# Two attention layers on one core: layer 1's q and k by seven products of quarters in 20 of 24 head pairs

## The chip, the cores and the metric

The kernel runs on one core of one Trainium2 chip. The metric is the device time of one execution in microseconds, the median of three runs. All data are 32-bit floats in SBUF; matrix products and the adds that make their inputs are in this type too.

## The reference, cut to what matters

Two layers run one after the other on an image batch of 4 x 32 x 32 tokens and 768 channels (12 heads of 64). Each normalizes its input by groups, computes q, k and v for every token, attends over all 1024 tokens with two position biases, projects, and adds the result to its input. Layer 1 also convolves q, k and v with a 3x3 depthwise kernel and normalizes each head:

```python
qkv = x @ w_qkv.T + b_qkv
q, k, v = (qkv[0], qkv[1], qkv[2])          # per head, H x W x 64
q = layer_norm(dwconv3x3(q, w_pool_q), g_q, b_q)
k = layer_norm(dwconv3x3(k, w_pool_k), g_k, b_k)
v = layer_norm(dwconv3x3(v, w_pool_v), g_v, b_v)
attn = einsum('bqc,bkc->bqk', q * scale, k) + rel_h[..., None] + rel_w[..., None, :]
o = softmax(attn) @ v + q
x = x + o @ w_proj.T + b_proj
```

The change is in the first line, for q and k of layer 1 alone.

## The kernel before

**Stages and pairs.** A stage is one batch image in one layer. The eight stages run in the order: layer 0 of images 0 and 1, layer 1 of images 0 and 1, then the same for images 2 and 3 (L170). A stage has six pairs of heads (hp 0 to 5), so there are 48 items; items 12 to 23 and 36 to 47 are layer 1. A pair fills 128 partitions, two heads of 64. Tokens are cut in two halves of 512.

**Steps.** `attend` (L735) is the frame. For one pair it goes through two halves of queries, and in each through two groups of four key tiles. A group computes four score tiles "s" (L915 for q and k, L917 for the position bias), ScalarE takes the exponentials "e" (L922), and then TensorE multiplies them with the values ("av", L939). It yields twice after the scores and twice after av, so one pair's attention has 16 steps: steps 0, 1, 4, 5, 8, 9, 12, 13 come after scores, the others after av. All other work is tied to steps by the table `events` (L1088): `plan` (L650) gives each pair's pieces with a step relative to the attention of the pair before it, and negative steps lie in the attention two before. At one step, pieces of earlier pairs come first. Each engine works its queue strictly in this program order.

**Layer 1's preparation of a pair** (L682 to L724): `padded` computes one half of q, k or v by 12 matmuls of 64 columns (`product`, L469; `halves`, L134, splits 128 columns in two; each matmul is two instructions in the profile) and ScalarE copies it with its bias into a padded image (two copies, L534). q's halves come at steps -7 (-8 for hp 1 and 4) and -6, k's at -4 and -2, v's at 2 and 4. VectorE (DVE) then convolves with nine taps (L549 the first, L551 the others): q's taps at steps -4 to 0, k's at 2 to 6, v's at 8 to 11. `centre` (L553; q at 3, k at 8, v at 13) transposes on TensorE ("ln_c"), and DVE subtracts the mean (L566, L567). `norm` (q at 7 or 8, k at 12, v at 15) takes the reciprocal root on ScalarE (L159, L161) with a step of Newton on DVE (L163 to L166) and multiplies (L589); for v the result is "vt", which av reads. `back` (q at 9, k at 14) transposes again ("ln_t") and ScalarE writes q and k. `positions` (L605, steps 10 and 11) computes the position terms "rel", and ScalarE copies them; `split` (L631, step 12) makes the bias out of them: ScalarE rounds (L636), DVE takes the rest (L637), and GpSimd sends 16 DMAs (L647).

**PSUM.** Eight banks: two for the first and fourth score tiles, one for av, one small bank, and two places of two banks, left ("b") and right ("c"), that hold the second and third score tiles. Other work takes single banks from the places in a fixed turn: after scores left, left, right, right; after av right, right, small, left, left (L118, L125). A new tile waits until all readers of what lay there are done.

**Weights and DMA.** `load_weights` (L247) has two buffers; `used` (L271) asks for the use after the next when one is done, on the queue of SyncE (SP). The order of uses is the list `uses` (L223).

**Products by sevens** exist already in layer 0 (`sevens`, L398) and in the projections (`four` and `three`), with sums of weights made once by DVE (`mix_weights`, L274) and kept in DRAM ("mixed").

**Projection and group norm.** The projection of a stage runs inside the first attention of the next, on steps 9 to 19 when layer 1 follows (L1138). The group norm of the next stage (L312) runs at given steps after the first of the stage before (L1099).

Of the kernel before, what the change touches and what calls it, by code (L numbers as in the profile page):

```python
# [51 lines left out]
def two_layers(ctx: ExitStack, tc: tile.TileContext, keep, x_in, wqkv, wproj, rels, windows, vrow, small, const, onehot, picks, out):  # L52
# [81 lines left out]
    def halves(ps, a, b, start=True, stop=True, **kw):  # L134

        for lo in (0, D):
            nc.tensor.matmul(ps[lo : lo + D], a[:, lo : lo + D], b, start=start, stop=stop, **kw)  # L137
# [37 lines left out]
    def rows(x):  # L175
# [3 lines left out]
    weights = {}  # L179

    N_SUMS = 5
    V_SUMS, PROJ_SUMS = NC, NC + NC // 2
    mixed = [
        dram.tile([P, N_SUMS, NC // 2, P], F32, tag=f"mixed{u}", name=f"mixed{u}")
        for u in range(PROJ_SUMS + 2 * (NC // 2))
    ]
    mixed_there = set()


# [19 lines left out]
    def in_sevens(i):  # L209

        return items[i][1] == 0 and i >= 2

    def shift(i):

        return 4 if i and items[i][1] == 0 and items[i - 1][1] == 1 else 0
# [8 lines left out]
    for i, (_, layer, hp) in enumerate(items):  # L224
        first = (i - 1) * 16 + shift(i)
        if in_sevens(i):
            uses += [(first, (i, 0, 0)), (first + 0.1, (i, 0, 1)), (first + 2, (i, 0, 2)), (first + 2.1, (i, 0, 3))]
            if hp % 2 == 0:
                uses += [(first + 8, (i, 2, 0)), (first + 8.1, (i, 2, 1)), (first + 10, (i, 2, 2)), (first + 10.1, (i, 2, 3))]
        else:  # L230
            uses += [(first + r, (i, s)) for s, r in enumerate((-8, -4, 2) if layer else (0, 4, 8))]
    uses = [use for _, use in sorted(uses)]
# [14 lines left out]
    def load_weights(n):  # L247

        if n >= len(uses):
            return  # L250
        i, s, *some = uses[n]
        _, layer, hp = items[i]
        w = wp.tile([P, NC, P], F32, tag="wqkv", name="wqkv_t")
        weights[uses[n]] = w
        if not some:
            nc.sync.dma_start(w, wqkv[layer, hp, :, s])
        elif some[0] == 0:
            (pa, sa), (pb, sb) = two(i, s)
            nc.sync.dma_start(w[:, :3, :], wqkv[0, pb, :, sb, 3:])
            nc.sync.dma_start(w[:, 3:, :], wqkv[0, pa, :, sa, :3])  # L260
        else:
            load_sums(w, hp if s == 0 else V_SUMS + hp // 2, some[0])
# [11 lines left out]
    def mix_weights(u):  # L274


        a = wp.tile([P, NC, P], F32, tag="wproj", name="mix_a")
        b = wp.tile([P, NC, P], F32, tag="wproj", name="mix_b")
        if u < PROJ_SUMS:
            (pa, sa), (pb, sb) = two(u, 0) if u < V_SUMS else two(2 * (u - V_SUMS), 2)  # L280
            nc.sync.dma_start(a, wqkv[0, pa, :, sa])
            nc.sync.dma_start(b, wqkv[0, pb, :, sb])
        else:
            layer, m = divmod(2 * (u - PROJ_SUMS), NC)
            for i, w in enumerate((a, b)):
                nc.sync.dma_start(w, wproj[layer, :, :, m + i, :].rearrange("h p q -> p h q"))
        yield
        a1, a2, b1, b2 = a[:, :3, :], a[:, 3:, :], b[:, :3, :], b[:, 3:, :]
        for n, to, x, y, op in (
            (2, None, a1, b2, ALU.add), (4, None, b1, a1, ALU.subtract), (0, b1, b1, b2, ALU.add),  # L290
            (1, a1, a1, a2, ALU.add), (3, a2, a2, b2, ALU.subtract),
        ):
            if to is None:
                to = wp.tile([P, HALF], F32, tag="x", name="mix")
                to = to[:, : 3 * P].rearrange("p (n c) -> p n c", c=P)
            nc.vector.tensor_tensor(to, x, y, op)
            nc.sync.dma_start(mixed[u][:, n], to)
        mixed_there.add(u)
        yield

    def mix_tokens(stage):


        x11, x12, x21, x22 = (xns[stage][:, n : n + 3, h : h + HALF] for n in (0, 3) for h in (0, HALF))
        for to, x, y, op in (
            (quarters[2], x21, x22, ALU.add), (x21, x21, x11, ALU.subtract), (quarters[1], x11, x12, ALU.add),
            (x12, x12, x22, ALU.subtract), (quarters[0], x11, x22, ALU.add),
        ):
            nc.vector.tensor_tensor(to, x, y, op)
            yield  # L310

    def group_norm(stage):  # L312
# [69 lines left out]
    class Pair:  # L382
# [9 lines left out]
        def column(self, s):  # L392
            return BIAS[self.layer] + 6 * s + self.hp

        def make_vt(self):
            self.vt = work.tile([P, NKT, P], F32, tag="vt", name="vt")

        def sevens(self, s, second):  # L398

# [107 lines left out]

        def put_k(self, ps, h, scale, bias):
            if self.k is None:
                self.k = work.tile([P, T], F32, tag="k", name="k")  # L510
            nc.scalar.activation(self.k[:, h * HALF : (h + 1) * HALF], ps, AF.Identity, bias=bias, scale=scale)

        def plain(self, s, h):
# [10 lines left out]
        def padded(self, s, h):  # L524

            if h == 0:
                self.pad[s] = in_turn("pad", pads)
            ps = self.product(s, h)
            ps = ps.rearrange("p (a c) -> p a c", a=S)

            for g, own, there in ((h, slice(0, S // 2), 1), (1 - h, slice(-1, None) if h == 0 else slice(0, 1), 0 if h == 0 else S // 2 + 1)):
                src = ps[:, :, own]
                rows = slice(g * (S + 2) + 1, g * (S + 2) + 1 + S)
                nc.scalar.activation(  # L534
                    self.pad[s][:, rows, there : there + src.shape[2]], src, AF.Identity, bias=col(self.column(s))
                )

        def taps(self, s, lo, hi):

            n_rows = 2 * S + 2  # L540
            if lo == 0:

                self.y[s] = in_turn("y", convolved)
            y = self.y[s].rearrange("p (a c) -> p a c", c=S // 2)
            for t in range(lo, hi):
                window = self.pad[s][:, t // 3 : t // 3 + n_rows, t % 3 : t % 3 + S // 2]
                tap = col(TAPS + 9 * s + t)
                if t == 0:
                    nc.vector.tensor_scalar(y, window, tap, None, ALU.mult)  # L549
                else:  # L550
                    nc.vector.scalar_tensor_tensor(y, window, tap, y, ALU.mult, ALU.add)  # L551
# [98 lines left out]
        def plan(self):  # L650
# [14 lines left out]
            if not self.layer:  # L665
# [15 lines left out]

            late = self.hp in (0, NC // 2)  # L682
            early_late = self.hp in (1, NC // 2 + 1)
            pieces = [
                (-8 if early_late else -7, lambda: self.padded(Q, 0)),
                (-6, lambda: self.padded(Q, 1)),
                (-4, lambda: self.padded(K, 0)),
                (-2, lambda: self.padded(K, 1)),
                (2, lambda: self.padded(V, 0)),
                (4, lambda: self.padded(V, 1)),  # L690
                (3, lambda: self.centre(Q)),
# [19 lines left out]

            taps = (
                (Q, -4, (2, 2, 2, 2, 1)),
                (K, 2, (2, 2, 2, 2, 1)),
                (V, 8, (2, 2, 3, 2)),
            )
            for s, r, counts in taps:
                lo = 0
                for n in counts:
                    some = lambda s=s, lo=lo, n=n: self.taps(s, lo, lo + n)  # L720
                    some.taps = True
                    pieces.append((r, some))
                    r, lo = r + 1, lo + n
# [371 lines left out]
    for k in range(1, len(stages)):  # L1095
        first = (k - 1) * NC * n_steps
        at(first + n_steps + 4, lambda k=k: load_xn(stages[k]))
        norm = group_norm(stages[k])
        for r in (34, 37, 41, 41, 48, 48, 52, 55, 58, 61, 64) if stages[k - 1][1] else range(34, 70, 3):  # L1099
            at(first + r, lambda norm=norm: next(norm, None))  # L1100
        if stages[k][1] == 0:
            mix = mix_tokens(stages[k])
            for r in range(5):
                step = 5 * n_steps + r // 3 if stages[k - 1][1] else 4 * n_steps + 4 + r // 2
                at(first + step, lambda mix=mix: next(mix, None))
        elif stages[k - 1][1] == 0:
            at(first + 4 * n_steps + 6, lambda: [nc.gpsimd.memset(pad, 0.0) for pad in pads])
# [3 lines left out]

    for u, call, step in (
        (2, 0, 5), (7, 6, 11), (3, 13, 18), (4, 22, 29), (8, 31, 38), (5, 40, 47), (0, 49, 55), (6, 57, 63), (1, 65, 71),
        (9, 72, 77), (10, 78, 83), (11, 84, 89), (12, 124, 135), (13, 137, 147), (14, 149, 159),
    ):
        mix = mix_weights(u)
        for at_step in (call, step):
            at(at_step, lambda mix=mix: next(mix))
# [6 lines left out]
    for k, stage in enumerate(stages):  # L1125
# [6 lines left out]
            continue  # L1132
        at(first + 2, call)
        late = stages[k + 1][1]
        for r, what in ((1, (0,)), (6, (1,)), (8, (2,)), (9, (3,)), (10, (4,))) if late else ((4, (0, 1)), (5, (2,)), (6, (3,)), (8, (4,))):
            at(first + r, lambda sums=sums, what=what: sums(what))

        for r, n in zip((9, 11, 13, 15, 17, 19) if late else (7, 9, 11, 13, 14, 15), (2, 1) * 3):  # L1138
# [339 lines left out]
```

## Time and profile before

| | |
|---|---|
| median of three runs | 3781.18 us (3780.49 to 3783.07) |
| profiled execution | 3784.75 us |
| its span, first to last instruction | 3783.0 us |
| granted TensorE clock | 0.998 |
| PE (TensorE) busy | 3730.7 us, 99% |
| DVE busy | 2397.2 us, 63% |
| ACT (ScalarE) busy | 1654.9 us, 44% |
| POOL (GpSimd) busy | 624.9 us, 17% |
| one pair of layer 1, 1323.8 to 1396.3 | 72.5 us: PE 72.5, DVE 55.6, ACT 36.2 |

The profile is one execution. Rows of groups give line, engine, operation, what is written from what, shapes and count; then busy time and the mean of one in ns; then the engine's idle time ahead of these instructions and who ended it. Timeline rows give start, duration, engine, line and operation, and idle time before in brackets. PEld is TensorE's loading of weights, which overlaps its matmuls. "Busy" of PE is modelled from pipelined matmuls.

### The profile page before, as it was taken

To read this page: it belongs to the slowest core of one execution; us is meant where nothing else is said; L and a number is where in the kernel's file an instruction comes from. 1 tells how busy PE (TensorE), PEld (TensorE's weight loads), DVE (VectorE), ACT (ScalarE), POOL (GpSimd) and SP (SyncE) were. 2 spreads that over 40 slices of the span, in tenths; PEclk is the share of its full clock that TensorE was granted. 3 is DMA by queue.
4 is the path that set the end of the run, shared out by engine and by line. 5 is a ranking of instruction groups with operands and counts; after the bars stand their busy time and mean duration, and the time that the engine had idled before them with its cause. 6 is when DMAs were issued, how large, how long until landed. Compare 5 with 4: busy or idle time off the path is not lost.

```text
span 3783.0 us, 77367 instructions
## 1 busy us (share of the span) xinstructions
PE 3730.7 (99%) x33166; PEld 1655.8 (44%) x33166; DVE 2397.2 (63%) x3069; ACT 1654.9 (44%) x2338; POOL 624.9 (17%) x1152
## 2 busy tenths in 40 slices
PE   8999999999999999999999999999999999999998
PEld 4535535534344444444535445355343444434442
DVE  2566554559678777688444554445686787867774
ACT  2455424545245443345424544254442554524551
POOL 0111100110122221122300010011111122111230
PEclk9999999999999999999999999999999999999999
DMA  4444543431431223411344232523224222142123
GB/s 149 115 134 124 144 143 102 113 90 46 123 100 48 64 57 94 127 49 47 88 120 128 62 86 67 182 68 86 55 54 142 71 64 58 47 127 66 47 59 101
DMA packets 209166, 345.08 MB, mean 91 GB/s; under 512 B 36982, under 2 KB 93202, under 8 KB 208816
## 3 DMA queue, kind: packets, MB, share of 16 engines
q1 hardware_dynamic: 130832, 224.84, 19.2%
q0 software_dynamic: 77984, 115.21, 13.1%
q8 instruction: 264, 4.33, 0.5%
q14 instruction: 86, 0.70, 0.1%
HBM read 195.95 MB, written 43.09 MB: 63 GB/s over the span
## 4 chain that ended last, share of the span: by engine, by line
PE 91%; DVE 5%; issue 1%; DMA 1%; ACT 1%; POOL 0%; SPq 0%; DVEq 0%; ACTq 0%; POOLq 0%
PE qkv L137 20%; PE s L915 17%; PE av L939 16%; PE m1m L137 5%; PE m4m L137 4%; PE m3m L137 4%; PE s L917 4%; PE p4p L137 3%; PE p3p L137 3%; PE rel L620 3%; PE p1p L137 3%; PE m L137 2%; PE ln_c L563 2%; PE p L137 1%; DVE acc L933 1%
## 5 line engine op out<-in xcount | busy, mean ns | idle before, releaser
L922 ACT ACTIVATE e<-s 128x1024 f32<-128x1024 f32 x768 | 775.3, 1023 | 407.7 <-PE s L917 377.8
L137 PE MATMUL qkv<-xn,wqkv_t 128*64 128x512 f32 x3648 | 814.4, 595 | 4.5 <-PE ln_t L598 2.4
L915 PE MATMUL s<-q,k 64*128 64x512 f32 x3072 | 809.0, 603 | 2.8 <-ACT e L922 1.9
L551 DVE SCALAR_TENSOR_TENSOR shared<-shared,sm 128x1056 f32<-128x1056 f32 x576 | 757.2, 1315 | 14.5
L917 PE MATMUL s<-bias,ones 64*128 64x512 f32 x1536 | 614.7, 791 | 1.4 <-issue 0.7
L939 PE MATMUL av<-e,vt 128*64 128x512 f32 x2624 | 597.9, 597 | 0.0
L647 POOL DMA_DIRECT2D bias<-high x384 | 203.5, 552 | 1750.7 <-ACT high L636 1484.0
L137 PEld LDWEIGHTS qkv<-xn,wqkv_t 128*64 128x64 f32 x3648 | 256.2, 137 | 479.8 <-issue 465.7
L933 DVE TENSOR_TENSOR acc<-acc,e 128x1024 f32<-128x1024 f32 x294 | 360.1, 1225 | 123.0 <-ACT e L922 96.1
L915 PEld LDWEIGHTS s<-q,k 64*128 64x128 f32 x3072 | 280.0, 186 | 260.7 <-issue 217.3
L534 ACT ACTIVATE shared<-qkv,sm 128x512 f32<-128x512 f32 (+1 forms) x288 | 129.0, 501 | 546.1 <-PE qkv L137 528.3
L939 PEld LDWEIGHTS av<-e,vt 128*64 128x64 f32 x2624 | 186.3, 137 | 349.6 <-issue 314.1
L917 PEld LDWEIGHTS s<-bias,ones 64*128 64x128 f32 x1536 | 149.8, 187 | 183.6 <-issue 180.8
L647 POOL DMA_DIRECT2D bias<-whole x384 | 206.9, 569 | 25.5 <-DVE whole L637 14.8
L762 ACT COPY weighed<-av 128x512 f32<-128x512 f32 x96 | 56.3, 587 | 307.8 <-PE av L939 307.8
L931 DVE TENSOR_TENSOR acc<-e 128x1024 f32<-128x1024 f32 x49 | 60.0, 1224 | 165.4 <-PE z L837 126.2
L566 DVE TENSOR_REDUCE mean<-ln_c 128x8 f32<-128x512 f32 x144 | 98.6, 685 | 101.1 <-PE ln_c L563 101.1
L780 POOL DMA_DIRECT2D inv<-z_inv x94 | 55.2, 592 | 592.1 <-DVE z_inv L774 543.9
L620 PEld LDWEIGHTS rel<-q,rel 64*32 64x32 f32 x6144 | 111.9, 105 | 60.6 <-issue 56.5
L620 PE MATMUL rel<-q,rel 64*32 64x32 f32 x6144 | 122.6, 195 | 1.9 <-issue 1.9
L620 PE MATMUL rel<-q_t,rel 64*32 64x32 f32 x6144 | 123.6, 195 | 0.2 <-issue 0.2
L419 DVE TENSOR_TENSOR shared<-shared,m3m 128x512 f32<-128x512 f32 x66 | 45.3, 687 | 121.7 <-PE m3m L137 121.7
(177 smaller groups left out, 4312.1 us busy)
## 6 DMA issues: line engine op xcount, KB each, us to landing
bias<-high POOLq DMA_DIRECT2D x384, 128.0 KB, 2.9
bias<-whole POOLq DMA_DIRECT2D x384, 128.0 KB, 3.1
wqkv_t<-in_wqkv SPq DMA_DIRECT2D x78, 384.0 KB
wqkv_t<-mixed SPq DMA_DIRECT2D x66, 384.0 KB
wproj_t<-mixed SPq DMA_DIRECT2D x48, 384.0 KB
wqkv_t<-in_wqkv SPq DMA_DIRECT2D x66, 192.0 KB
xn<-in_x SPq DMA_DIRECT2D x24, 512.0 KB
x<-in_x SPq DMA_DIRECT2D x48, 256.0 KB
```

What stands on the lines that cost most here:

```text
L137: nc.tensor.matmul(ps[lo : lo + D], a[:, lo : lo + D], b, start=start, stop=stop, **kw)
L534: nc.scalar.activation(self.pad[s][:, rows, there : there + src.shape[2]], src, AF.Identity, bias=col(self.column(s)))
L551: nc.vector.scalar_tensor_tensor(y, window, tap, y, ALU.mult, ALU.add)
L563: nc.tensor.transpose(ps[:, t * P : (t + 1) * P], y[:, tokens], ident)
L566: nc.vector.tensor_reduce(of, heads, AX.X, ALU.add)
L620: nc.tensor.matmul(ps[lo : lo + S, k * S : (k + 1) * S].rearrange("p (b c) -> p b c", b=2), rel[rows, 2 * self.layer + i, first : first + ...
L647: nc.gpsimd.dma_start(sets, some.unsqueeze(1).to_broadcast([D // 2, 2, QC]))
L915: nc.tensor.matmul(ps[:, j, :], k[rows, keys], q[rows, cols], start=True, stop=False)
L917: nc.tensor.matmul(ps[:, j, :], ones[rows, kt % 2 * P : (kt % 2 + 1) * P], bias[c][rows, kt // 2, :], start=False, stop=True,)
L922: nc.scalar.activation(e, ps, AF.Exp)
L933: nc.vector.tensor_tensor(acc, acc, e, ALU.add)
L939: nc.tensor.matmul(av[j * D : (j + 1) * D, :], pair.vt[:, kt, j * D : (j + 1) * D], e[:, j, :], start=(kt == 0), stop=(kt == NKT - 1),)
```

## The change

For the 20 items of layer 1 whose two predecessors are layer 1 too (14 to 23, 38 to 47), q and k of a pair, both token halves, are computed together by seven products of quarters (in Strassen's manner, the form with few additions): a term is 6 matmuls, half a `padded` product. `products(0)` to `products(3)` stand where the four `padded` stood. The terms are w1, w6, (w2,) w7, w4 for q's halves, w5 and w3 for k's. Four inputs are sums of tokens (S1 to S4), made once per stage by DVE (`sum_tokens`, 12 additions of 512 columns and as many stores of 256 KB) and kept in DRAM; each pair calls each of them back, three blocks of 256 KB, into one set of buffers right after the term that read the set before. Sums of weights for the six pairs are made once (six more units of `mix_weights`, in layer 0).

The results are put together by DVE, partly in PSUM (w4, w5 and w3 get their terms added in place), before ScalarE pads them as before (`put_from` is the second half of `padded`). The first tap of k and v is done by ScalarE, at steps 1 and 6. The buffers vt and k have one place each in layer 1 now; the blocks and temporaries lie in those that layer 0 uses. The group norms ahead of layer 1 run some 10 steps earlier, and the mixing of weights is put at other steps.

The core of the diff:

```diff
+    def in_products(i):
+        return all(items[k][1] == 1 for k in (i, i - 1, i - 2))
...
+        elif in_products(i):
+            uses += [(first + r, (i, 0, n)) for n, r in enumerate((-8, -6.5, -6, -2))] + [(first + 2, (i, 2))]
         else:
             uses += [(first + r, (i, s)) for s, r in enumerate((-8, -4, 2) if layer else (0, 4, 8))]
...
+        elif layer and some[0] < 2:
+            nc.sync.dma_start(w[:, :3, :], wqkv[layer, hp, :, 0, 3 * some[0] : 3 * some[0] + 3])
+            nc.sync.dma_start(w[:, 3:, :], mixed[LATE_SUMS + hp][:, some[0]])
+        elif layer and some[0] == 3:
+            nc.sync.dma_start(w[:, :3, :], wqkv[layer, hp, :, 1, 3:])
+        elif layer:
+            load_sums(w, LATE_SUMS + hp, some[0])
...
+        if u >= LATE_SUMS:
+            t1, t2 = (
+                wp.tile([P, HALF], F32, tag="x", name="mix")[:, : 3 * P].rearrange("p (n c) -> p n c", c=P) for _ in range(2)
+            )
+            for n, to, x, y in ((3, t1, b1, a1), (0, t2, b2, t1), (1, b1, b2, b1), (2, a2, a2, t2)):
+                nc.vector.tensor_tensor(to, x, y, ALU.subtract)
+                nc.sync.dma_start(mixed[u][:, n], to)
+            mixed_there.add(u)
+            yield
+            return
...
+    def sum_tokens(stage):
+        for n in range(NC // 2):
+            x11, x12, x21, x22 = (xns[stage][:, n + k, h : h + HALF] for h in (0, HALF) for k in (0, 3))
+            def keep_sum(which, x, y, op):
+                to = wp.tile([P, HALF], F32, tag="x", name="token_sum")
+                nc.vector.tensor_tensor(to, x, y, op)
+                nc.sync.dma_start(tokens[stages.index(stage) % 2][which, n], to)
+                return to
+            s1 = keep_sum(S1, x21, x22, ALU.add)
+            s2 = keep_sum(S2, s1, x11, ALU.subtract)
+            yield
+            keep_sum(S4, x12, s2, ALU.subtract)
+            yield
+            keep_sum(S3, x11, x21, ALU.subtract)
...
+            self.vt = one.tile([P, NKT, P], F32, tag=self.home("vt"), name="vt")
...
+        def call(self, which):
+            if which == S2:
+                two_blocks = one.tile([P, 2, HALF], F32, tag="vt0", name="blocks")
+                third_block = work.tile([P, 2, QC], F32, tag="acc", name="third_block", bufs=1)
+                self.blocks = [two_blocks[:, 0], two_blocks[:, 1], third_block[:, 0]]
+            for n, block in enumerate(self.blocks):
+                nc.sync.dma_start(block, tokens[stages.index((self.b, self.layer)) % 2][which, n])
+        def seven(self, ps, at, x, more=False):
+            w = weights[self.i, 0, at // 2][:, 3 * (at % 2) : 3 * (at % 2) + 3, :]
+            for n in range(3):
+                halves(ps, w[:, n, :], x[n], start=not (n or more), stop=n == 2, skip_group_check=True)
+        def second(self):
+            self.seven(self.w12, 2, [xns[self.b, self.layer][:, 3 + n, :HALF] for n in range(3)], more=True)
+            self.put_from(0, 0, self.w12)
+        def products(self, n):
+            Q, K = 0, 1
+            xn = xns[self.b, self.layer]
+            x = {(h, k): [xn[:, 3 * k + n, h * HALF : (h + 1) * HALF] for n in range(3)] for h in range(2) for k in range(2)}
+            add = lambda to, x, y: nc.vector.tensor_tensor(to, x, y, ALU.add)
+            early = self.hp in (1, NC // 2 + 1)
+            if n == 0:
+                temps = one.tile([P, 2, HALF], F32, tag="k0", name="temps")
+                self.u, self.x = temps[:, 0], temps[:, 1]
+                self.pad[Q] = in_turn("pad", pads)
+                self.w12, w6 = bank("w1w2"), bank("w6")
+                self.seven(self.w12, 0, x[0, 0])
+                nc.scalar.copy(self.u, self.w12)
+                self.seven(w6, 1, self.blocks)
+                used((self.i, 0, 0))
+                self.call(S3)
+                if early:
+                    self.second()
+                add(self.u, self.u, w6)
+            elif n == 1:
+                w7 = bank("w7")
+                if not early:
+                    self.second()
+                self.seven(w7, 3, self.blocks)
+                used((self.i, 0, 1))
+                self.call(S1)
+                add(self.x, self.u, w7)
+                w4 = bank("w4")
+                self.seven(w4, 4, x[1, 1])
+                add(w4, w4, self.x)
+                self.put_from(Q, 1, w4)
+            elif n == 2:
+                self.pad[K] = in_turn("pad", pads)
+                w5 = bank("w5")
+                self.seven(w5, 5, self.blocks)
+                used((self.i, 0, 2))
+                self.call(S4)
+                add(self.u, self.u, w5)
+                add(w5, w5, self.x)
+                self.put_from(K, 1, w5)
+            else:
+                w3 = bank("w3")
+                self.seven(w3, 6, self.blocks)
+                used((self.i, 0, 3))
+                add(w3, w3, self.u)
+                self.put_from(K, 0, w3)
+                after = self.i + 1
+                if after < len(items) and in_products(after) and items[after][2]:
+                    pairs[after].call(S2)
...
-                if t == 0:
+                if t == 0 and hi == 1:
+                    nc.scalar.activation(y, window, AF.Copy, scale=tap)
...
+            if in_products(self.i):
+                steps = (-8 if early_late else -7, -6, -4, -2)
+                pieces = [(r, lambda n=n: self.products(n)) for n, r in enumerate(steps)]
+                if not (self.hp and in_products(self.i - 1)):
+                    pieces.insert(0, (-10, lambda: self.call(S2)))
...
-                (K, 2, (2, 2, 2, 2, 1)),
-                (V, 8, (2, 2, 3, 2)),
+                (K, 2, (2, 2, 2, 2)),
+                (V, 8, (2, 2, 2, 2)),
             )
+            pieces += [(1, lambda: self.taps(K, 0, 1)), (6, lambda: self.taps(V, 0, 1))]
             for s, r, counts in taps:
-                lo = 0
+                lo = 0 if s == Q else 1
...
-        for r in (34, 37, 41, 41, 48, 48, 52, 55, 58, 61, 64) if stages[k - 1][1] else range(34, 70, 3):
+        if stages[k][1]:
+            places = (24, 26, 29, 29, 32, 32, 36, 39, 42, 45, 48) if stages[k - 1][1] else range(27, 60, 3)
+            token_sums = sum_tokens(stages[k])
+            for r in range(9):
+                at(first + 4 * n_steps - 2 + r, lambda token_sums=token_sums: next(token_sums))
```

In the order of DVE's instructions after the change, the two additions at w5 stand behind L637 and ahead of q's first tap, and the one at w3 stands behind L799 and ahead of two q taps and v's norm.

## Prediction

> **What bounds the kernel now.** I read the page first, then the groups with shapes kept apart, the engines' busy time in three stretches of one pair of layer 1, and last the timelines of TensorE (PE) and VectorE (DVE) in the stretch that looked tightest. From the page, the engines:
>
> ```profile
> span 3783.0 us, 77367 instructions
> ...
> PE 3730.7 (99%) x33166; PEld 1655.8 (44%) x33166; DVE 2397.2 (63%) x3069; ACT 1654.9 (44%) x2338; POOL 624.9 (17%) x1152
> ```
>
> PE is idle for only 52 us. From the groups, the product that is replaced, and a DVE addition from PSUM like those that are added:
>
> ```profile
> L137 PE MATMUL qkv<-xn,wqkv_t 128*64 128x512 f32 x3648 | 814.4, 595 | 4.5 <-PE ln_t L598 2.4 <-DVE shared L567 1.1 <-DVE xn L356 0.9
> L419 DVE TENSOR_TENSOR shared<-shared,m3m 128x512 f32<-128x512 f32 x66 | 45.3, 687 | 121.7 <-PE m3m L137 121.7
> ```
>
> Now one pair's period, in three stretches: from the first q product to the end of the scores before the first k product; from the norm of the previous pair's k to that of its v; from there on to the next pair.
>
> ```profile
> core 0: us, PE busy (x) PEld busy (x) DVE busy (x) ACT busy (x) POOL busy (x), PEclk, DMA share, GB/s
> 1292.40:1313.90 21.50, 21.50 (x350) 10.22 (x350) 14.04 (x15) 12.03 (x17) 3.32 (x6) 1.00 0.14 35
> 1315.40:1333.90 18.50, 18.50 (x96) 7.43 (x94) 17.35 (x27) 8.29 (x15) 9.46 (x18) 1.00 0.56 136
> 1334.60:1365.00 30.40, 30.40 (x156) 12.46 (x156) 20.76 (x26) 13.30 (x19) 4.61 (x8) 1.00 0.10 24
> ```
>
> PE is full in all three, but in the second DVE is busy 17.35 of 18.50 us. There the two engines are bound together. The timelines, DVE first:
>
> ```profile
> 1315.44 0.18 DVE L163 TENSOR_TENSOR t_ln<-r_ln 128x16 f32<-128x16 f32 x1 [8.43 <-ACT r_ln L161]
> ...
> 1322.65 0.69 DVE L567 SCALAR_TENSOR_TENSOR shared<-mean,ln_c 128x512 f32<-128x512 f32 x1
> ...
> 1331.75 0.18 DVE L163 TENSOR_TENSOR t_ln<-r_ln 128x16 f32<-128x16 f32 x1 [0.53 <-ACT r_ln L161]
> ...
> 1332.59 1.22 DVE L589 TENSOR_TENSOR vt<-shared,r_ln 128x1024 f32<-128x1024 f32 x1
> ```
>
> ```profile
> 1313.86 5.37 PE L137 MATMUL qkv<-xn,wqkv_t 128*64 128x512 f32 x24
> 1319.16 1.09 PE L563 MATMUL ln_c<-cst,shared 128*128 128x128 f32 x8
> 1320.19 3.65 PE L939 MATMUL av<-e,vt 128*64 128x512 f32 x16
> 1323.77 1.09 PE L598 MATMUL ln_t<-cst,shared 128*128 128x128 f32 x8
> 1324.79 5.37 PE L137 MATMUL qkv<-xn,wqkv_t 128*64 128x512 f32 x24
> ...
> 1334.65 1.94 PE L939 MATMUL av<-e,vt 128*64 128x512 f32 x8
> ```
>
> The scores end at 1313.93; ScalarE (ACT) finishes the exponentials and the reciprocal root (L161), and from 1315.44 DVE works without a pause, but for the 0.53 us, until vt is written at 1333.81. PE's av at 1334.65 reads that vt: 0.84 us of slack. The same interval in the 16 pairs of layer 1 that have no projection in this stretch is 18.4 us (19.9 in three, with part of a group norm in it), and the slack 0.83 to 1.21 (0.21 in those three); their mean is about 0.8.
>
> **The change part by part.** *Matmuls.* A half product is 24 instructions, 5.37 us; one of the seven is 12, so 2.69. Per pair 4 x 5.37 - 7 x 2.69 = 2.7 us less, 54 us in 20 pairs. (By the m rows of the existing sevens, 120.8/528 = 0.229 us an instruction against 0.223, it is 44.) But it isn't even: q takes five terms (13.4 for 10.7: **+2.7**) before the scores, k two (5.4 for 10.7: -5.4), both inside the DVE-bound stretch.
>
> *DVE.* Six additions per pair at 0.687: one for w6, two at w7 and w4, two at w5, one at w3. Writing back into PSUM has no row; the same shape costs 683 ns SBUF to SBUF (L1006) and 750 with two operations from PSUM (L1022); I take 687. The instruction order puts both w5 additions after L637 and before the first q tap, and w3's after L799: three, 2.06 us, inside the stretch. The taps that go to ACT (L549, 764 ns, two per pair) are those of k and v, at steps 1 and 6: **outside** it. So DVE needs 18.38 + 2.06 = 20.4 us from L163 to vt, against PE's own work from the end of the scores to av of 20.72 - 5.4 = 15.3. L163 follows the scores' end by 1.5 as now, since it waits on the same four exponentials. Av therefore comes 1.5 + 20.4 + 0.1 = 22.1 us after the scores, not 20.7: **+1.3** (2.06 less the 0.8 slack). PE waits first at the second ln_t, whose bank DVE's L567 must have read; queued behind are w3 and the next scores. Then ACT's root for v stands ahead of four exponentials on its queue, so the fourth score tile and av wait.
>
> *A bank.* The second "rel" of positions moves from the small bank to the left pair, which the second score tile takes. Its copies (0.58 + 1.03) now stand on ACT behind the two pad copies of w4 (0.9), and those behind DVE's addition (0.7). From w4's end that is 0.1 + 0.7 + 0.9 + 1.6 = 3.35 us, while PE gets there after rel 1.3 and one tile 1.1: **+1.0** (0 if ACT were quick, 2 if DVE is still on taps; DVE has about 8 us idle there, so I take 1.0).
>
> Third stretch: PE's work is unchanged, DVE has 10 us idle and loses two taps there: 0. So an exposed pair changes by 2.7 + 1.0 + 1.3 = +5.0 us, 16 x 5.0 = **+80**. In the other four (hp 2 of each stage) the projection lies in the stretch, with 19 to 21 us of slack before av: there PE's saving counts, 4 x -2.7 = **-11**.
>
> *Group norm and sums ahead.* For the two stages whose predecessor is layer 1, the last bn_stats (4 x 0.68) and a normalization (2 x 0.8) land at step 13 of pairs that had none, one such leaves, and three token sums (0.68) fall on steps 14 and 15: 2.8 + 1.6 - 1.6 + 2.0 = 4.8 each, **+10** in all. The other sums (48 in all, 33 us) and six more weight mixes lie where DVE has slack: 0, and 10 us at most if that cover is gone.
>
> *Transfers.* 240 block loads of 256 KB, 48 stores: 75 MB. SP's queue moved 224.84 MB in 19.2% of 3783 us, 309 GB/s, so 6% of the span. S3 is called 8 us of PE's work ahead of its use (av, last, positions, one term), S1 as long (w4, positions, scores); 384 KB of weights and 768 KB of blocks take 1.1 to start, as an issue at 1308.19 whose bytes moved from about 1309.2, and 3.8: hidden. S4 is the tight one, see below. The one vt and one k of layer 1 cost nothing: their readers on PE end 9 to 10 us before they are rewritten. ACT gains 1.06 (as L573) twice and one copy, in idle time.
>
> Sum: 80 - 11 + 10 = +79 on the profiled 3784.75 (span 3783.0 and 1.75 around it), which is 3.6 above the median: 3781.2 + 79 = **3860**.
>
> *A rule against a row.* The Trainium skill (Perfetto Trace Analysis, Identifying the Most-Contended Engine) calls occupancy a fair measure for VectorE and says to optimize the engine with the highest occupancy first. By that, DVE at 63% has room, and the change earns its 44 to 54 us: 3730. The stretch's row, 17.35 of 18.50, says the room is in other stretches of the same pair, which a queue worked in order can't use. I go by the row.
>
> **Rivals.**
> A. *PE stays the bound* (faster). All is hidden, and the 54 us come: 3727 to 3737. For it: PE 99%, and 8 us of DVE idle before L163. Against: that idle waits for exponentials that come after the scores. It needs DVE's stretch to be shorter than PE's 15.3 by some reordering, and the order shows none. 7%.
> B. *S4 comes late* (slower still). Its 768 KB go out behind v's 384 KB when w5 ends, just as GpSimd sends 2.1 MB of bias (16 issues of 128 KB in 8.4 us; DMA share 0.56). The skill (DMA: Bandwidth & Descriptors, Queues, rings and completion order) has each engine take turns between queues with work: half of 309 gives 7.6 us + 1.1 to start, under the 8.8 until w3 may begin after ln_t's new wait: nothing. If bias went first, 1.1 + 9 + 3.8 = 13.9, against 10.6 when the last block is needed: 3.3 us late, 0.6 of it covered by DVE, 16 x 2.7 = 43: 3903. No row shows the two queues so. 12%.
> C. *Only the shift of PE's work* (milder). The bank costs nothing and the moved pieces find gaps: 16 x (2.7 + 1.3) - 11 = 53: 3834. 18%.
> D. *It breaks even*: DVE's additions and bank cost nothing and k's gain still doesn't show: 3775 to 3788. 3%.
>
> **Numbers.** Main case 60%, 3845 to 3880. A measurement of this kernel can tell about 0.2% (7.6 us) from no change. Slower: 60 + 12 + 18 = 90%; same 3%; faster 7%. The range takes in B and C with their bounds, 3822 to 3905, and leaves out A, D and the tails.
>
> **What would show it.** Right: PE's idle time up from 52 to 150-200 us though its busy time falls by 45 to 54; waits of ln_t on L567 grow from 4.6 to some 50; av and s wait on vt and on ACT's exponentials in layer 1; DVE stays near 95% from the k norm to the v norm, and that interval reads 20.4; periods of 77 to 78 us for 72.5. Wrong: a period below 72.5, with av waiting for nothing (A); PE waiting on DMA for "blocks" at w3 (B); no wait at the second score tile (C).

## The result and the profile after

The changed kernel takes 3934.64 us (median of four runs, 3933.65 to 3940.7) against 3781.59 for the kernel before on the same chip: a ratio of 1.0406 (95% interval 1.0394 to 1.0419), 153 us slower. The direction was forecast, the size was not: 3860 was predicted, and the range ended at 3905. The profiled execution took 3933.7 us.

From the page, span and engines:

```profile
span 3931.9 us, 77953 instructions
...
PE 3744.4 (95%) x32926; PEld 1645.2 (42%) x32926; DVE 2481.9 (63%) x3213; ACT 1705.6 (43%) x2406; POOL 620.8 (16%) x1152
```

PE's idle time (span less busy) went from 52.3 to 187.5 us, as forecast (150 to 200). But PE has 240 instructions less and is busy 13.7 us *longer*, where 45 to 54 us less was forecast. That is the first sign of what the forecast lacked. Now the list of PE's waits (total, how often, the longest), first of the kernel before and then of the changed one:

```profile
PE ln_t L598 <- DVE shared L567: 4.6, 7, 0.8
...
PE p1p L137 <- DVE os_sums L1027: 3.3, 3, 1.1
...
PE s L915 <- ACT e L922: 1.9, 2, 1.0
```

```profile
PE ln_t L734 <- DVE shared L703: 57.7, 20, 5.7
PE s L1060 <- ACT e L1067: 47.2, 19, 3.8
PE p1p L137 <- DVE os_sums L1172: 14.1, 8, 2.9
...
PE s L1060 <- ACT whole L762: 12.1, 16, 0.8
PE p3p L137 <- DVE os_sums L1172: 6.0, 5, 1.5
```

L703 is what was L567 (the subtraction of `centre`), L734 `back`, L1060 and L1067 scores and exponentials, L762 the copy of "rel". The three forecast waits are there (first, second and fourth row): the first and the fourth once in each of the 16 exposed pairs, the second in 12 of them. The rows of p1p and p3p, the projection's products, were not forecast.

One pair in the three stretches of the prediction, and a fourth row for the 3.4 us after the second ln_t:

```profile
core 0: us, PE busy (x) PEld busy (x) DVE busy (x) ACT busy (x) POOL busy (x), PEclk, DMA share, GB/s
1332.90:1357.95 25.05, 24.27 (x360) 10.70 (x360) 15.22 (x17) 12.48 (x18) 3.33 (x6) 1.00 0.34 101
1359.50:1381.10 21.60, 16.14 (x74) 6.32 (x70) 19.21 (x29) 8.47 (x15) 9.59 (x18) 0.92 0.81 208
1381.20:1410.30 29.10, 29.10 (x152) 12.05 (x150) 20.06 (x21) 15.03 (x20) 4.41 (x8) 1.00 0.09 25
1368.78:1372.20 3.42, 3.42 (x10) 1.40 (x12) 3.35 (x4) 1.72 (x2) 2.47 (x5) 0.51 1.06 224
```

The first stretch grew by 3.55 us: 2.8 of PE's work and a wait of 0.76 at the second score tile. In the second, from the k norm to the v norm, PE's work has shrunk to 16.1 us and it waits for DVE, which is at work for 19.2 of 21.6. The third is unchanged: from av to the next q product 29.06 us, before 29.05. The last row is new: the clock stands at 0.51. PE's timeline there:

```profile
1365.32 0.66 PE L734 MATMUL ln_t<-cst,shared 128*128 128x128 f32 x4
1368.78 1.03 PE L734 MATMUL ln_t<-cst,shared 128*128 128x128 f32 x4 [2.81 <-DVE shared L703]
1369.74 3.17 PE L137 MATMUL w<-blocks,wqkv_t 128*64 128x512 f32 x8
1372.75 1.02 PE L137 MATMUL w<-third_block,wqkv_t 128*64 128x512 f32 x4
1373.70 1.13 PE L1060 MATMUL s<-q,k 64*128 64x512 f32 x4
```

The second ln_t waits 2.81 us for DVE, and the term behind it, w3, takes 4.0 us to the start of the next matmul (1369.74 to 1373.70), where w6, as many instructions, takes 2.6 at full clock (1335.52 to 1338.09). DVE's timeline shows who pays for that:

```profile
1359.56 0.17 DVE L163 TENSOR_TENSOR t_ln<-r_ln 128x16 f32<-128x16 f32 x1 [3.60 <-ACT r_ln L161]
...
1362.68 0.68 DVE L626 TENSOR_TENSOR temps<-temps,w 128x512 f32<-128x512 f32 x1
1363.28 0.69 DVE L626 TENSOR_TENSOR w<-w,temps 128x512 f32<-128x512 f32 x1
...
1371.85 0.75 DVE L944 SCALAR_TENSOR_TENSOR q<-t,sm,q 128x512 f32<-128x512 f32 x1
1373.83 0.70 DVE L626 TENSOR_TENSOR w<-w,temps 128x512 f32<-128x512 f32 x1 [1.22 <-PE w L137]
1374.43 2.67 DVE L687 SCALAR_TENSOR_TENSOR shared<-shared,sm 128x1056 f32<-128x1056 f32 x2
...
1379.80 1.22 DVE L725 TENSOR_TENSOR vt<-shared,r_ln 128x1024 f32<-128x1024 f32 x1
```

The three rows of L626 are the additions at w5 and w3. DVE, which sets the pace, itself waits 1.22 us for the slowed w3. From the scores' end to av it is 23.3 us where 22.1 were forecast; this wait is about the difference.

From here on, attention n is that of item n, from its first score tile to the next item's. The exposed pairs are prepared in attentions 13 to 17, 19 to 21, 37 to 41 and 43 to 45, the four with a projection in 12, 18, 36 and 42. Attention 17, which holds the end of the stretch above, takes 78.5 us for 72.5: +6.0 where +5.0 was forecast. Over the 16 exposed attentions it is +2.2 to +12.4.

The whole 148.9 us of the two spans: PE idle +135.2, time lost to a lower clock (the length of each stretch times one less the clock granted in it) +58.0, from 8.4 to 66.4; the remainder, -44.3, is less matmul work, and agrees with the 44 that the prediction took from the m rows.

### The profile page after: what moved, and what is told of

It reads as the page before. It is cut to its first block, busy times and chain, and to the rows that moved or that the text cites. A ratio compares the mean times of both kernels' runs of the same rounds, so it can differ in the third digit from the quotient of the medians.

```text
span 3931.9 us, 77953 instructions
## 1 busy us (share of the span) xinstructions
PE 3744.4 (95%) x32926; PEld 1645.2 (42%) x32926; DVE 2481.9 (63%) x3213; ACT 1705.6 (43%) x2406; POOL 620.8 (16%) x1152
## 3 DMA queue, kind: packets, MB, share of 16 engines
q1 hardware_dynamic: 189008, 321.60, 26.1%
## 4 chain that ended last, share of the span: by engine, by line
PE 77%; DVE 13%; ACT 4%; issue 2%; DMA 2%; POOL 0%; SPq 0%; DVEq 0%; ACTq 0%; POOLq 0%
PE av L1084 14%; PE s L1060 13%; PE qkv L137 9%; PE w L137 6%; PE m1m L137 4%; PE m3m L137 4%; PE m4m L137 4%; PE s L1062 3%; DVE shared L687 3%; PE w1w L137 3%; PE p3p L137 3%; PE p4p L137 2%; PE p1p L137 2%; PE m L137 2%; PE rel L756 2%
## 5 line engine op out<-in xcount | busy, mean ns | idle before, releaser
L1067 ACT ACTIVATE e<-s 128x1024 f32<-128x1024 f32 x768 | 768.5, 1023 | 407.6 <-PE s L1062 382.5
L1060 PE MATMUL s<-q,k 64*128 64x512 f32 x3072 | 818.8, 609 | 61.8 <-ACT e L1067 47.2
L1084 PE MATMUL av<-e,vt 128*64 128x512 f32 x2624 | 607.2, 605 | 0.1
L1060 PEld LDWEIGHTS s<-q,k 64*128 64x128 f32 x3072 | 278.5, 187 | 336.3 <-issue 209.4
L137 PE MATMUL qkv<-xn,wqkv_t 128*64 128x512 f32 x1728 | 384.7, 594 | 0.9 <-DVE xn L407 0.9
L137 PEld LDWEIGHTS qkv<-xn,wqkv_t 128*64 128x64 f32 x1728 | 120.2, 137 | 233.3 <-issue 226.4
L783 POOL DMA_DIRECT2D bias<-whole x384 | 207.1, 567 | 21.6 <-DVE whole L773 11.1
L592 ACT ACTIVATE shared<-qkv,sm 128x512 f32<-128x512 f32 (+1 forms) x128 | 57.3, 501 | 278.3 <-PE qkv L137 273.5
L137 PE MATMUL w<-blocks,wqkv_t 128*64 128x512 f32 x640 | 174.0, 668 | 0.0
L925 POOL DMA_DIRECT2D inv<-z_inv x94 | 52.3, 561 | 651.5 <-DVE z_inv L919 435.7
L592 ACT ACTIVATE shared<-w,sm 128x512 f32<-128x512 f32 x120 | 53.8, 501 | 226.5 <-DVE w L626 226.5
```

Source lines behind the costliest of these rows:

```text
L592: nc.scalar.activation(self.pad[s][:, rows, there : there + src.shape[2]], src, AF.Identity, bias=col(self.column(s)))
L783: nc.gpsimd.dma_start(sets, some.unsqueeze(1).to_broadcast([D // 2, 2, QC]))
L1060: nc.tensor.matmul(ps[:, j, :], k[rows, keys], q[rows, cols], start=True, stop=False)
L1067: nc.scalar.activation(e, ps, AF.Exp)
L1084: nc.tensor.matmul(av[j * D : (j + 1) * D, :], pair.vt[:, kt, j * D : (j + 1) * D], e[:, j, :], start=(kt == 0), stop=(kt == NKT - 1),)
```

## The experiments

Twelve kernels. The theory after the result (T): the waits at ln_t and at the fourth score tile come from DVE's chain, as forecast; many of them throw PE to half clock afterwards, and that is what the forecast lacked. The rivals: the low clock is a mere sign of the waits and costs nothing by itself; the transfers (B of the prediction); the bank.

**Work in the gaps.** Matmuls that nobody reads are put ahead of the second ln_t and the fourth score tile.

```diff
+    def fill(pair):
+        ps = small_bank("fill")
+        for _ in range(3):
+            halves(ps, ident, xns[pair.b, pair.layer][:, 0, :HALF])
...
+            if (s, h) == (1, 1) and exposed(self.i):
+                fill(self)
...
+                    if (c, kt) == (0, 3) and exposed(pair.i):
+                        fill(pair)
```

> The changed kernel with three pairs of dummy matmuls (128x64 by 512 columns, 2.7 us) put where TensorE waits in layer 1, before the second ln_t of k and before the fourth score tile of the first group; their result is not used. Theory (DVE's chain makes TensorE idle, and each idle of 2.7 us is followed by a window at half the TensorE clock): the waiting stays but is filled, the lost clock falls from 66 us to under 20, time 3934 to 3870-3895. Rival 1 (the low clock costs nothing that matters, the waits alone are the loss): 3930-3945. Rival 2 (blocks come late by DMA): 3930 or more, as the filled gaps were not the cause.

Measured: 3895.19, ratio 1.0299 (1.0282 to 1.0316). More work, and 39 us less time. The answer on the clock, of this kernel and of the changed one:

```profile
core 0: 3892.0 us, clock 0.997
```

```profile
core 0: 3931.9 us, clock 0.983
```

The clock's loss falls from 66.4 to 11.7 us, and attention 17 to 77.2: with the clock held it is about what was forecast (72.5 + 5.0). DVE's wait for w3, 1.0 to 2.6 us in nine exposed attentions, is left in one. The fill takes no other work away, so the half clock is shown to be a cost by itself, not a sign of the waits.

**The k additions left out** (two at w5, one at w3; k is then not the reference's).

```diff
-                add(self.u, self.u, w5)
-                add(w5, w5, self.x)
...
-                add(w3, w3, self.u)
```

> The changed kernel without the three DVE additions at w5 and w3, so that k's halves are single terms and not the sums (part of the computation is left out). Theory (DVE's chain from the norm of k to the norm of v): three times 0.69 us and the wait for a slowed w3 leave it, about 3.3 us in each of 16 pairs and fewer low-clock windows: 3855-3890. Rival (late blocks by DMA): the same loads remain, 3925 or more.

Measured: 3850.23, ratio 1.0177 (1.0160 to 1.0194), 84 us less. That is below the expected range: more was gained than expected. DVE's busy time falls by only 36.4 us; PE's idle time falls by 47.7 and the clock's loss by 35.9. Part of it is in a place not forecast: the four attentions with a projection, +21.5 us together in the changed kernel, are at +4.2, and PE's waits at p1p and p3p in them fall from 19.3 to 5.8 us.

**The calls of S3, S1 and S4 left out** (180 loads, 47 MB; w7, w5 and w3 then multiply the blocks of S2).

```diff
-                self.call(S3)
...
-                self.call(S1)
...
-                self.call(S4)
```

> The changed kernel without the calls of S3, S1 and S4: w7, w5 and w3 multiply the blocks of S2 again, so 180 block loads (47 MB) are left out and the products are not those wanted. Theory (DVE's chain): no change but for chance, 3920-3940. Rival (blocks come late, or their traffic delays the bias): the loss goes, 3780-3860.

Measured: 3937.27, ratio 1.0406 (1.0388 to 1.0423): no change. Rival B falls; the calls of S2 and the stores of the sums remain in this kernel.

**The bank of w4**, and with it "rel" back in the small bank.

```diff
-                w4 = bank("w4")
+                w4 = place_b.single("w4") if self.hp != 2 else bank("w4")
```

> The changed kernel with w4 in the left place and the second rel back in the small bank, so that the second score tile waits for w4's pad copies and not for rel's copies behind them (not for hp 2). Theory: the 0.76 us wait at the second score tile goes, and the chain starts about as much earlier: 16 pairs, 10 to 20 us less, 3912-3925. Rival (this bank is the main loss): under 3880.

Measured: 3922.83, ratio 1.0371 (1.0354 to 1.0388), 12 us less. The wait on L762 (12.1 us) disappears from the list. A real term of the forecast's size (1.0 a pair forecast, 0.76 measured), and not the main one.

**Room in DVE's chain.** k's norm one step earlier, ahead of the additions, and the q and k taps moved out of the stretch.

```diff
-                (12, lambda: self.norm(K)),
...
-                (Q, -4, (2, 2, 2, 2, 1)),
-                (K, 2, (2, 2, 2, 2)),
+                (Q, -5, (2, 0, 1, 0, 3, 3)),
+                (K, 3, (2, 2, 2, 2)),
...
+            pieces.append((11, lambda: self.norm(K)))
```

> The changed kernel with DVE's work in layer 1 at other steps: the norm of k at step 11 behind v's taps (ahead of the exponentials, where DVE was idle), q's nine taps as 2 at step 11, 1 at step 13, 3 at step 15 behind v's norm, 3 at step 0, and k's taps a step later. Nothing is left out. Theory: some 8 us leave the chain, TensorE hardly waits and keeps its clock: 3770-3815. Rival (the terms themselves, their banks or their DMA are the loss): 3880 or more.

Measured: 3828.33, ratio 1.0124 (1.0107 to 1.0141), 106 us less, but above the expectation. Attention 17 takes 71.3, *below* the 72.5 of before. The kernel's waits show what is left:

```profile
PE p1p L137 <- DVE os_sums L1172: 19.8, 8, 4.7
...
PE s L1060 <- ACT e L1067: 9.2, 7, 2.7
PE ln_t L734 <- DVE shared L703: 7.8, 8, 2.2
```

The waits of s on the exponentials have fallen from 47.2 to 9.2 us and those of ln_t from 57.7 to 7.8; p1p, in attentions with a projection, has grown from 14.1 to 19.8.

**The same order in the kernel before**, to see what it costs without products (the edit is the same, with k's taps (2, 2, 2, 3)).

> The kernel before, with DVE's work at the steps of the third experiment's schedule (norm of k at step 11, q's taps 2, 1, 3, 3 at steps 11, 13, 15, 0, k's taps from step 3), and no products of quarters. Theory (TensorE is the bound there, DVE's chain only just fits): the same, 3770-3795. Rival (the schedule itself is worth what it gave to the changed kernel): 3700 or less.

Measured: 3820.35, ratio 1.0104 (1.0087 to 1.0120). A miss: the order isn't free. Regular pairs stay at 72.5; attentions 12, 18, 36 and 42, where the projection runs, lose 4.2 to 5.9 us each and the ones after them 1.9, where moved taps now stand ahead of the projection's additions on DVE. In each of the four PE waits 2.2 us at ln_t for a norm's multiplication (L589) and 1.6 us at p1p for the projection's sums. With the old order left in these four (the third kernel of the next group but one) they lose 0.6 or nothing: it is the order there that costs. How much of it is the taps and how much the norm was not separated.

**Order, bank, and the group norm and token sums moved off the stretch** together, in 20 pairs and then in 16 (hp 2 of each stage left out, whose preparation lies beside a projection).

```diff
-        return all(items[k][1] == 1 for k in (i, i - 1, i - 2))
+        return items[i][2] != 2 and all(items[k][1] == 1 for k in (i, i - 1, i - 2))
```

> The schedule of the third experiment on the changed kernel, with w4 in the left place, and with the token sums between two layer 1 stages at steps 1 to 9 of the fourth pair and the group norm's pieces of step 13 at step 12, where DVE waits. Nothing is left out. Theory: 0.8 us in 16 pairs and about 5 us in each of the two attentions that held the sums: 3790-3812. Rival (these places cost nothing): 3828.

> The same, with the products of quarters in 16 pairs only: the pair prepared during a projection (hp 2 of each layer 1 stage) keeps its four plain products. Theory (in that attention DVE serves the projection and the terms, and TensorE waits 4 to 5 us for it at p1p, while the terms save 2.7): 12 to 25 us less than with 20 pairs, 3770-3795, level with the kernel before. Rival (there the saving of TensorE counts in full): 10 us more.

Measured: 3820.33, ratio 1.0100 (1.0084 to 1.0117), and 3807.04, 1.0070 (1.0053 to 1.0086). Both above the expectation, but their difference of 13 us is in the range given for it (12 to 25). In the kernel with 16 pairs regular attentions are at 70.7, 1.8 us under the kernel before, but single ones give it back: 12 and 36 lose 2.9 each, 13 and 37 lose 3.5 and 5.2, 18 and 42 4.8 and 3.9, 15 and 39 (where the token sums now stand) 5.2 each.

**The order only where no projection runs; sums by GpSimd or DVE; the same order in the kernel before.** The first two have 16 pairs and w4's bank as above, the group norm near its old steps, and the mixing of weights moved; they differ from each other only in the engine of the sums.

```diff
+    def apart(a):
+        return a >= 0 and items[a][1] == 1 and items[a][2] != 0
...
-                nc.vector.tensor_tensor(to, x, y, op)
+                nc.gpsimd.tensor_tensor(to, x, y, op)
```

> The products kept in 16 pairs, the early norm of k and the moved taps only where the attention runs no projection, the group norm ahead of layer 1 near its old steps, the token sums by GpSimd at steps where they are due late. My theory (after the 16 pairs with the new order for DVE stood at 3807: what they still lost lies in single attentions, 5.8 us in 12 and 36, 8.7 in 13 and 37, 8.7 in 18 and 42, 10.4 in 15 and 39, 6.5 in 9 and 11, all from DVE work put into the wrong steps): 3807 less most of these 40 us, 3762 to 3785. Rival (the products cost these attentions their time wherever DVE's work is put, so that they break even at best): 3795 to 3810.

> The same with the token sums left to DVE, at the same steps. If DVE's room in those attentions is what counts: 3 to 12 us more than with GpSimd, 3768 to 3795. If GpSimd takes as much from DVE as it does for it: the same within 2 us, or less than with GpSimd.

> The kernel before with the same early norm of k and moved taps in the same attentions, without products. My theory (the new order costs time only where a projection runs): the kernel before within 6 us, 3776 to 3790. Rival (the order costs or gains by itself): off by more, as the 3820 of the same order in all attentions.

Measured: 3790.3, ratio 1.0021 (1.0013 to 1.0029), with GpSimd; 3810.82, 1.0078 (1.0064 to 1.0092), with DVE; 3791.9, 1.0032 (1.0020 to 1.0044), the kernel before in this order. The first two are above the expectation, and their difference of 20 us is more than the 3 to 12 given: with DVE, attentions 15 and 39 lose 17 us each, 12 to 13 of it PE's idle time. A term that was not forecast shows there: DVE stands idle ahead of a sum until the store of an earlier one has landed and freed its buffer (there are two), 6.8 and 9.0 us in these two attentions. In the list of DVE's waits:

```profile
DVE token_sum L354 <- DMA tokens<-token_sum: 36.7, 15, 4.9
```

In the changed kernel these waits are 16.4 us in all. With GpSimd this wait falls on GpSimd. The third kernel is 2 us outside its own expectation: attentions 14, 20 and 38 lose 1.1 each, and thirteen others 0.4 to 0.6.

**Products in 12 pairs**, where neither the group norm nor a projection is near, and the group norm at its old steps.

```diff
-        return items[i][2] != 2 and all(items[k][1] == 1 for k in (i, i - 1, i - 2))
+        return items[i][2] > 2 and all(items[k][1] == 1 for k in (i, i - 1, i - 2))
...
+            places = (34, 37, 41, 41, 48, 48, 52, 55, 58, 61, 64) if stages[k - 1][1] else range(34, 67, 3)
```

> Products in 12 pairs alone (the fourth to the sixth pair of each layer 1 stage), the group norm at its old steps, token sums by GpSimd once it is done, the early norm of k only in attentions 13 to 15, 19 to 21 and their like, no more mixing of weights beside an older one. The 16 pairs with GpSimd's sums stood at 3790, having gained 1.7 to 2.2 us in attentions 13, 17, 19, 37, 41, 43, 44 and 45 each, and lost 8.6 in 15 and 39, 4.6 in 14 and 38, 4.8 in 16 and 40, 6.6 in 18 and 42. My theory (these losses are the group norm's earlier place and the sums beside it, in 18 and 42 the q taps of the next pair; what the identity saves stays): 12 us of gains in 13, 19, 37, 43, 44, 45, 1 to 3 more in 14, 20, 21 and 38, no loss elsewhere: 3765 to 3777. Rival (the products have to be paid for somewhere in any order): 3779 to 3790.

Measured: 3780.22, ratio 0.9994 (0.9986 to 1.0003): no difference from before that can be told, which is what the rival gave. The expected gains came: attentions 13, 19, 37 and 43 gain 2.1 each, 44 and 45 1.8 each, 14, 15, 20, 21, 38 and 39 0.7 to 0.8 each, 16.6 us in all. But 16, 17, 40 and 41 lose 13.8 together. No product is prepared in these four, and GpSimd makes token sums in them; PE waits there for DVE, 0.9 to 1.5 us at a time. Attention 9 loses 4.2, whose cause is open. DVE's timeline beside one of these sums, and GpSimd's:

```profile
1287.67 0.17 DVE L164 TENSOR_TENSOR t_ln<-t_ln,lnv 128x16 f32<-128x16 f32 x1
1287.88 1.65 DVE L165 TENSOR_SCALAR t_ln<-t_ln 128x16 f32<-128x16 f32 x1
1289.56 0.17 DVE L166 TENSOR_TENSOR r_ln<-r_ln,t_ln 128x16 f32<-128x16 f32 x1
1289.77 2.18 DVE L728 TENSOR_TENSOR shared<-shared,r_ln 128x1024 f32<-128x1024 f32 x1
```

```profile
1288.21 1.28 POOL L354 TENSOR_TENSOR token_sum<-xn,token_sum 128x512 f32<-128x512 f32 x1
1289.56 1.31 POOL L354 TENSOR_TENSOR token_sum<-xn 128x512 f32<-128x512 f32 x1
```

L165 takes 0.17 us elsewhere and ends here at 1289.53, just after GpSimd's first sum; L728 takes 1.22 elsewhere. (L165 is recorded as starting 0.33 us ahead of that sum; the profile's spans on GpSimd are rough.) GpSimd's sum holds up DVE: instructions of DVE beside one of the 48 sums are lengthened by 36 us in all (30 in the kernel with 16 pairs), where the sums themselves would take DVE 33 us (48 x 0.69). So it doesn't take the work off DVE; what it spares DVE is the wait for the stores. No version was found that is faster than the kernel before by more than the runs can tell.

## Why the prediction was wrong

*The step that failed* is the pricing of the pairs. In "an exposed pair changes by 2.7 + 1.0 + 1.3 = +5.0 us" every microsecond of wait was priced at one microsecond, and the low clock behind it at nothing. In "there PE's saving counts, 4 x -2.7" a second place of waiting was left out. The 16 exposed attentions cost 119 us where 90 were forecast (80, and 10 for group norm and sums), the four with a projection +21.5 where -11 was forecast, and the rest 8.5, within the 10 at most that was allowed for it. The clock's loss in the exposed attentions is 52.9 us, and the miss in the four is 32.5. It took both to leave the range, which ends at 3905: without the clock's loss the total would be about 3882 (the kernel with filled gaps measures 3895), and had the four come as forecast, 3902.

1. *Matmuls*, 44 to 54 us less: right at 44.3 (the remainder above), with +2.8 of PE's work ahead of the scores.
2. *The bank*, +1.0: 0.76, right, and 12 us less without it.
3. *DVE's chain*, right in mechanism: the additions cost 0.68 to 0.70 each (0.687 taken), PE waits first at the second ln_t, then at the fourth score tile. From L163 to vt it reads 21.5 us for 20.4; 1.22 of it is the wait for the slowed w3.
4. *Missing: the clock.* 52.9 of its 58.0 us fall in the exposed attentions. Without them these would have cost 119.0 - 52.9 = 66; with the gaps filled they measure 83.7 (that the fill is longer than some gaps is only argued). Either is under the forecast 90: the waits themselves were not priced too low. The Trainium skill (TensorE: Matmul & The Clock Gate, HAM oscillation — how this bites in real kernels) warns of PE-idle gaps above some 3.4 us. By that, the changed kernel's 7 such gaps would cost about 7 x 1.7 = 12 us (estimate, half clock for one window of 3.41 us each). The low stretches behind these 7 cost 20.5 us, since five of them last two windows; the other 32.4 us in the exposed attentions stand behind shorter gaps, so the measurement decides.
5. *Missing: the projection.* The forecast looked at the slack before av alone. In that stretch PE also waits for DVE at p1p and p3p, and the k additions stand ahead of those sums on DVE. These two waits make 19.3 of the 26.1 us by which PE's idle time grows in the four (the kernel before has neither there). Without the k additions they are 5.8, and the four at +4.2. That this is still 15 above the forecast -11 is explained only in part: another 4.8 us of PE's waits there are for ScalarE's exponentials.
6. *Transfers*, nothing: right, shown by leaving 47 MB out. The first taps by ScalarE were not undone by themselves; that they cost nothing is only argued. Nor were the group norm and the sums undone by themselves, so their +10 is not shown.

There was luck in the idle time: of its rise of 135.2 us, inside the forecast, 26.1 lie in the four pairs where a gain was forecast.

## What to carry to other kernels

Price a wait of the engine that bounds the kernel twice: by its length, and by what its clock loses afterwards. Before buying matmul time with additions, look at the one stretch where the adding engine is already full, and at *every* consumer behind it in its queue there, not just at the one that ends the stretch. An identity that saves a few per cent of a full engine pays only once its inputs' sums have a place that is free; here 0.7 to 2.1 us per attention could be had, 16.6 us in all, and the sums took 13.8 of them. Count with a sum what it waits for too: a store that must land before its buffer is free held up DVE in one of the kernels for longer than all its token sums took (36.7 us for 33).

## What the runs showed of the hardware

*The clock.* In every trace the stretches at half clock begin on one grid of 3.413 us, to within 0.03 us, and last one window or two (3.41 or 6.83 us), but for the one at the program's end. The 14 traces were cut on their grids (without the first 40 us; PE's idle time as the profile models it). All 150 windows in which PE was idle for 2.0 us or more were followed by a window at half clock; of those with 1.8 to 2.0 us 17 in 38 were, with 1.6 to 1.8 us 9 in 55, with less 32 in some 15,300, and each of these 32 was at half clock itself. So what counts in these traces is the idle time within a window, and a gap's place on the grid: above, 2.81 us lay in one window and cost half a window; the 2.66 us ahead of the fourth score tile (1377.24 to 1379.90) fell on a boundary (1.9 and 0.8), and the clock stayed at 1.00. The Trainium skill (same page, What's actually happening) has the free-running window of 3413 ns, but a whole idle window as what throttles; here 2.0 us of 3.41 sufficed every time.

*GpSimd beside DVE.* In the two kernels with sums by GpSimd (128x512 in SBUF, 1.27 to 2.36 us each), DVE's instructions beside a sum took up to 1.5 us longer, and up to 2.4 us beside two. The 11 TENSOR_REDUCEs beside a sum were not lengthened, and no DVE instruction away from the sums took over 0.3 us more than the median of its kind. The Trainium skill (SBUF — State Buffer, SBUF: two separate sides) calls the port they share an exclusive lock held for a whole instruction; the ends above agree.
